# Band attention: queries and keys transposed by Vector and transfers in place of TensorE, in a new order

## The chip, the cores and the metric

The kernel runs on one core of a Trainium2 chip. The metric is device time in microseconds (us), the median of several runs. Five engines work side by side, each through its own list of instructions in order: TensorE (PE in the profile; PEld is its weight load), VectorE (DVE), ScalarE (ACT), GpSimd (POOL) and SyncE (SP), which here only issues transfers (DMAs). They wait for each other through semaphores. SBUF is the working memory of 128 partitions; PSUM is the accumulator memory, eight banks of 2 KB per partition, where TensorE writes.

## The reference

The reference is a decoder of twelve stages over 32 sequences of 128 tokens with 128 features. Only the last stage changes. It is six layers of local attention, each followed by a gated feed-forward block:

```python
for i in range(DEPTH):                                   # 6
    x = attn_layer(shift_tokens(x), Wqkv[i], q_scale[i], k_scale[i], Wo[i]) + x
    x = ffn_layer(shift_tokens(x), ln_g[i], ln_b[i], W1[i], b1[i], W2[i], b2[i]) + x
```

In `attn_layer` the tokens are projected to queries, keys and values of 16 heads of 64; queries and keys are divided by their norms, scaled per feature and turned by rotary tables; each token attends to a band of its own window and the one before; the softmax of 8 times the scores weighs the values; the result is projected to 128 features. In `ffn_layer` a layer norm is followed by two projections to 341 columns, one passed through Gelu and multiplied with the other, and a projection back.

The score matmul contracts over the 64 features of a head, so queries and keys must lie with features on the partitions. The projections leave them with tokens on the partitions. They have to be transposed in between, and this step is what changes.

## The kernel before

The stage is `l3_ffn` of class `Fast` (from line 1818). An item n is one sequence in one layer: 6 x 32 = 192 items. The residual stream is `Z`, kept in SBUF throughout. The loop runs over t, and in each iteration every step works on another item: `steps` lists the functions with their lag, so that `(scores, 3)` in iteration t is the score step of item t - 3. The feed-forward block works on four items at once (a group g), so its functions in `blocks` come up in one of four iterations: `ff_gates` when t mod 4 is 0, `ff_up` and `ff_norm` when it is 1, `ff_down` and `ff_normed` at 2, `ff_turn` at 3. The text calls these four the gates, up, down and turn iterations; `shifted`, the transpose of the next four inputs, falls in the last. In the first layer the functions in `ahead` finish the stage before.

The order of the list is the order of the work on each engine. `Ordered` and `Lane` (lines 1332 to 1360) tie every compute instruction to the one before it on the same engine, so no engine overtakes; transfers are not tied. Every compute instruction goes through `Lane`, which is why the profile gives L1345 for all of them and groups have to be told apart by tile names.

The steps of an item are these, with the tile names that the profile shows.

- `queries(n, w)` multiplies the shifted input `zs` with 1024 columns of the weights, for queries (w = 0) and keys (w = 1), into a PSUM tile `qk`.
- `squares` squares it on ACT into `sq`; `summed` adds up the squares per head on DVE into `ss`. `sq` has one buffer.
- `swapped` and `rotated` read `qk` on DVE: one product with swapped halves into `rt`, one with the cosine table into `raw`; POOL adds the two in `raw`.
- `scaled`, an iteration later, makes the reciprocal roots of the sums (DVE, then 12 small POOL operations) and multiplies `raw` with them on POOL.
- `turned`, lag 2, transposes `raw` in 16 blocks of 128x128 on TensorE into PSUM tiles `rT`, four blocks to a tile; each tile is copied to SBUF as `qkT`, alternately by ACT and DVE. It stands in the list in two halves.
- `scores` fills two PSUM tiles `sc`. `hidden` first writes the band mask into all four banks of both with 16 small matmuls; 32 score matmuls add to it, and ACT takes the exponential into `P`.
- `valued` projects values (`vp`, copied to `va`); `values` multiplies `P` with them (`av`) and divides on DVE into `ao`; `features` transposes `ao` (`oTp`, then `oT`); `projected` multiplies with the output weights (`y`), and DVE adds to `Z`.
- `ff_norm` shifts by a matmul (`hp`), copies into `zh` and takes statistics; `ff_normed` normalises; `ff_turn` transposes (`xp`) into `xT`; `ff_gates` makes three projections (`gp`) and their Gelu (`g`); `ff_up` three more (`ap`) and the products `u`; `ff_down` projects back (`fy`).

PSUM is divided between two pools. The first holds three tiles of two banks for `qk`, `sc`, `av` and `vp`; the second two tiles of one bank for everything else. `zh` and `xT` are two names in one single buffer:

```python
p2 = es.enter_context(tc.tile_pool(name="L3fp2", bufs=3, space=PSUM))
p1 = es.enter_context(tc.tile_pool(name="L3fp1", bufs=2, space=PSUM))
...
zh = wk.tile([128, 4, 128], F32, tag="zh", name="zh", bufs=1)
...
xT = wk.tile([128, 512], F32, tag="zh", name="xT", bufs=1)
```

A tile of a pool is given its buffer when the last access to the buffer's former tile is over. Accesses of different engines to the same PSUM bank of one tile are kept apart, reads too. `weights` loads a layer's weights over SP's queue and builds the table `tab`.

Of the kernel before, what the change touches and what calls it, by code (L numbers as in the profile page):

```python
# [13 lines left out]
F32 = mybir.dt.float32  # L14
# [10 lines left out]
S = 128  # L25
# [1336 lines left out]
class Fast(General):  # L1362
# [455 lines left out]
    def l3_ffn(self):  # L1818
        if self.general:
            return super().l3_ffn()  # L1820
        tc, i, plain = self.tc, self.i, self.nc
        nc = self.nc = Ordered(plain, tc)
        N = DEPTH * NB
        with ExitStack() as es:
# [112 lines left out]

            def weights(l):
                wqkv = wt.tile([128, 3072], F32, tag="wqkv", name="wqkv")
                nc.sync.dma_start(out=wqkv, in_=i["dqkv"][l])  # L1940
                wo = wt.tile([128, 8, 128], F32, tag="wo", name="wo")
                nc.sync.dma_start(out=wo, in_=i["dwo"][l])
                w1 = wt.tile([128, 682], F32, tag="w1", name="w1")
                nc.sync.dma_start(out=w1, in_=i["dw1"][l])
                w2 = wt.tile([128, 3, 128], F32, tag="w2", name="w2")
                nc.sync.dma_start(out=w2, in_=i["dw2"][l])
                dqs = wt.tile([1, 256], F32, tag="dqs", name="dqs", bufs=1)
                nc.sync.dma_start(out=dqs, in_=i["dqs"][:, 256 * l:256 * l + 256])
                p = bank([128, 256], "tabp")
                mm(p, self.ones, dqs)  # L1950
                tab = wt.tile([128, 2, 2, 64], F32, tag="tab", name="tab")
                nc.vector.tensor_tensor(tab.rearrange("p w c d -> p (w c d)"), p, rot, ALU.mult)
                rs = wt.tile([128, NB, 16], F32, tag="rs", name="rs")
                W[l] = (wqkv, wo, w1, w2, tab, rs)

            def shifted(g):

                p = bank([128, 4, 128], "zT")
                for j in range(4):
                    turn(p[:, j, :], Z[:, 4 * (g % 8) + j, :])  # L1960
                zs = zs2[g % 2]
                nc.scalar.copy(zs[0:64], p[0:64])
                nc.vector.tensor_copy(zs[64:128, :, 1:128], p[64:128, :, 0:127])

            def queries(n, w):
                x = zs2[n // 4 % 2][:, n % 4, :]
                if w == 0:
                    S[n] = {"raw": wk.tile([128, 32, 64], F32, tag="raw", name="raw", bufs=3),
                            "ss": wk.tile([128, 32], F32, tag="ss", name="ss")}
                pp = banks([128, 16, 64], "qk")  # L1970
                for u in range(2):
                    c = 1024 * w + 512 * u
                    mm(pp[:, 8 * u:8 * u + 8, :], x, W[n // NB][0][:, c:c + 512])
                S[n]["qk"] = pp
# [30 lines left out]
                rn = self.rsqrt(wk, v, "s", nc.gpsimd)  # L2005
                nc.gpsimd.tensor_tensor(s["raw"], s["raw"], rn.unsqueeze(2).to_broadcast([128, 32, 64]), ALU.mult)

            def turned(n, us):
                s = S[n]
                flat = s["raw"].rearrange("p h d -> p (h d)")  # L2010
                if us[0] == 0:
                    s["qkT"] = wk.tile([128, 16, 128], F32, tag="qkT", name="qkT")
                for u in us:
                    p = bank([128, 4, 128], "rT")
                    for c in range(4):
                        o = 512 * u + 128 * c
                        turn(p[:, c, :], flat[:, o:o + 128])
                    (nc.vector.tensor_copy if u % 2 else nc.scalar.copy)(s["qkT"][:, 4 * u:4 * u + 4, :], p)

            def valued(n):  # L2020
                vp = banks([128, 16, 64], "vp")
# [4 lines left out]

            def scores(n):
                s = S[n]
                qkT = s["qkT"]

                sc = [banks([128, 2, 4, 128], "sc") for _ in range(2)]
                self.hidden(mm, [sc[f][:, e].rearrange("p c q -> p (c q)") for f in range(2) for e in range(2)],
                            self.bandT)
                s["P"] = []
                for f in range(2):
                    for c in range(4):
                        for e in range(2):
                            r = slice(64 * e, 64 * e + 64)
                            mm(sc[f][:, e, c, :], qkT[r, 8 + 4 * f + c, :], qkT[r, 4 * f + c, :], start=False, stop=c == 3)
                    P = wk.tile([128, 8, 128], F32, tag="P", name="P", bufs=4)  # L2040
                    nc.scalar.activation(P.rearrange("p h q -> p (h q)"), sc[f].rearrange("p e c q -> p (e c q)"), AF.Exp,
                                         scale=8.0)
                    s["P"].append(P)
# [40 lines left out]
            def ff_norm(g):  # L2084
                b = slice(4 * (g % 8), 4 * (g % 8) + 4)
                p = bank([128, 4, 64], "hp")
                mm(p, self.bg("shift"), Z[:, b, 64:128])
                zh = wk.tile([128, 4, 128], F32, tag="zh", name="zh", bufs=1)
                nc.gpsimd.tensor_copy(zh[:, :, 0:64], Z[:, b, 0:64])
                nc.scalar.copy(zh[:, :, 64:128], p)  # L2090
                mv = wk.tile([128, 4, 2], F32, tag="fmv", name="fmv")
                for j in range(4):
                    st = self.sp.tile([128, 6], F32, tag="bnst", name="bnst")
                    nc.vector.bn_stats(st, zh[:, j, :])
                    nc.vector.bn_aggr(mv[:, j, :], st)
                v = wk.tile([128, 4], F32, tag="fv", name="fv")
                nc.vector.tensor_scalar(v, mv[:, :, 1], EPS, None, ALU.add)
                rn = self.rsqrt(wk, v, "f", nc.gpsimd)
                nb = wk.tile([128, 4], F32, tag="fnb", name="fnb")
                nc.gpsimd.tensor_tensor(nb, mv[:, :, 0], rn, ALU.mult)  # L2100
                nc.gpsimd.tensor_scalar(nb, nb, -1.0, 0.0, ALU.mult, ALU.add)
                F[g] = {"xn": zh, "nb": nb, "rn": rn, "gs": [], "u": []}

            def ff_normed(g):
                zh, nb, rn = F[g]["xn"], F[g]["nb"], F[g]["rn"]
# [20 lines left out]
                    nc.scalar.activation(t[0:m], gp[0:m], AF.Gelu, bias=self.col(f"L3f_b1{l}1{c}")[0:m])  # L2126
                    F[g]["gs"].append((t, m))

            def ff_up(g):
                l = g // 8  # L2130
                w1, xT = W[l][2], F[g]["xT"]
                for c, (t, m) in enumerate(F[g]["gs"]):
                    ap = bank([128, 512], "ap")
                    mm(ap[0:m], w1[:, 128 * c:128 * c + m], xT)
                    u = uc if c == 2 else wk.tile([128, 512], F32, tag=f"u{c}", name=f"u{c}", bufs=1)
                    nc.vector.scalar_tensor_tensor(u[0:m], ap[0:m], self.col(f"L3f_b1{l}0{c}")[0:m], t[0:m],
                                                   ALU.add, ALU.mult)
                    F[g]["u"].append(u)

            def ff_down(g):  # L2140
# [10 lines left out]
                if l == DEPTH - 1:  # L2151
# [3 lines left out]

            weights(0)
            ahead = ((normed, 3), (x_values, 5), (x_scores, 6), (x_keys, 7), (x_turn, 8), (x_norm, 9), (x_root, 10))
            steps = ((features, 5), (summed, 1, 1), (scaled, 1), (queries, 0, 0), (squares, 0), (swapped, 0, 0),
                     (rotated, 0, 0), (turned, 2, (0, 1)), (scores, 3), (summed, 0, 0), (turned, 2, (2, 3)),
                     (queries, 0, 1), (squares, 0), (swapped, 0, 1), (rotated, 0, 1), (projected, 5), (values, 4))  # L2160
            blocks = ((ff_normed, 7), (ff_turn, 8), (ff_down, 11), (ff_up, 10), (ff_gates, 9), (ff_norm, 6))
            for t in range(-10, N + 12):
                if 0 <= t < N and t % NB == NB - 4 and t // NB + 1 < DEPTH:
                    weights(t // NB + 1)
                for fn, lag, *a in steps:
                    if 0 <= t - lag < N:
                        fn(t - lag, *a)
                for fn, lag in blocks:
                    n = t - lag
                    if n % 4 == 3 and 0 <= n < N:  # L2170
                        fn(n // 4)
                for fn, at in ahead:
                    n = t + at
                    if n % 4 == 0 and 0 <= n < NB:
                        fn(n // 4)
                if t % 4 == 3 and 0 <= t + 1 < N:
                    shifted((t + 1) // 4)
                if 0 <= t - 2 < N:
                    valued(t - 2)
# [888 lines left out]
```

## Time and profile before

| | |
|---|---|
| median of three runs | 6189.32 us (6188.6 to 6194.51) |
| the profiled execution | 6190.12 us |
| its span, first to last instruction | 6188.2 us |
| mean granted TensorE clock | 0.941 |
| the band layers, first query projection to the last | 2745 to 6094 us |

A line of the groups or of the timeline names the source line, the engine, the operation and the tiles as out<-in, then the shape and the count. In the groups, "busy, mean ns" follow, then the engine's idle time just before such instructions and what ended it. In the timeline the first two numbers are start and duration in us, and square brackets hold the idle time before. A line of the waits says who waited for whom, for how many us in total, how often, and the longest. In the table of windows each engine's busy time stands with its instruction count, then the granted clock.

Matmuls are pipelined: the start of the next one says how long one holds the engine, not its own duration. An fp32 matmul has two records per call.

### The profile page before, as it was taken

What the parts mean: (1) busy time and instruction counts of PE and PEld (TensorE: products, weight loads), DVE (VectorE), ACT (ScalarE), POOL (GpSimd) and SP (SyncE); (2) the same over time, 40 slices, a digit from 0 to 9 for tenths busy, and PEclk for the clock granted to TensorE, in tenths of its full rate; (3) what the DMA queues carried; (4) which work ended last, traced back from release to release, by engine and by line L of the source; (5) the groups of instructions that cost most, each with busy time, mean ns of one, the idle gap of its engine ahead of it and who ended that gap; (6) DMA issues with size and microseconds to landing.
All of it is one profiled execution on the core that took longest, in us unless ns stands there. A gap on an engine that the chain in (4) does not pass through costs nothing.

```text
span 6188.2 us, 144055 instructions
## 1 busy us (share of the span) xinstructions
PE 5484.6 (89%) x59686; PEld 3895.3 (63%) x59686; DVE 4046.0 (65%) x11606; ACT 2984.4 (48%) x4283; POOL 3083.4 (50%) x4828
## 2 busy tenths in 40 slices
PE   8867957868859999868999999999999999999998
PEld 4534546755646666646666666666666666666766
DVE  5576532345549999957666666666666676666664
ACT  6756611114435555524555554554555555554554
POOL 0141010011025555547766666666666667666774
PEclk9988966768989999989999999999999999999999
DMA  1000057533012212200000000000000000000000
GB/s 44 2 1 1 2 202 260 169 93 106 5 28 55 55 47 54 55 28 5 5 17 15 5 1 1 15 5 2 12 8 2 1 15 5 2 2 1 3 6 9
DMA packets 243639, 208.11 MB, mean 34 GB/s; under 512 B 125746, under 2 KB 230809, under 8 KB 237854
## 3 DMA queue, kind: packets, MB, share of 16 engines
q1 hardware_dynamic: 239372, 162.06, 9.1%
q0 software_dynamic: 2304, 33.56, 1.4%
q8 instruction: 471, 7.72, 0.5%
q10 hardware_dynamic: 1298, 3.19, 0.1%
q14 instruction: 194, 1.59, 0.1%
HBM read 140.83 MB, written 57.93 MB: 32 GB/s over the span
## 4 chain that ended last, share of the span: by engine, by line
PE 37%; DVE 21%; ACT 6%; issue 3%; POOL 1%; DMA 1%; SPq 0%; DVEq 0%; ACTq 0%; POOLq 0%
PE qk L1345 8%; DVE rt L1345 5%; PE vp L1345 5%; DVE raw L1345 5%; PE av L1345 5%; PE y L1345 5%; ACT sq L1345 4%; PE gp L1345 3%; PE fy L1345 2%; PE oTp L1345 2%; PE rT L1345 2%; DVE qkT L1345 2%; DVE ss L1345 1%; DVE ao L1345 1%; PE tp L1345 1%
## 5 line engine op out<-in xcount | busy, mean ns | idle before, releaser
L1345 POOL TENSOR_TENSOR raw<-raw,rt 128x1024 f32<-128x1024 f32 x384 | 902.6, 2356 | 335.1 <-DVE raw L1345 335.1
L1345 DVE TENSOR_TENSOR rt<-qk,tab 128x1024 f32<-128x1024 f32 x384 | 470.3, 1225 | 879.1 <-ACT sq L1345 869.7
L1345 POOL TENSOR_TENSOR raw<-raw,ry 128x2048 f32<-128x2048 f32 x224 | 811.3, 3622 | 17.5
L1345 PE MATMUL qk<-wqkv,zs 128*128 128x512 f32 x1536 | 728.0, 597 | 3.0 <-DVE zs L1345 3.0
L1345 ACT ACTIVATE sq<-qk 128x1024 f32<-128x1024 f32 x448 | 459.3, 1025 | 536.6 <-PE qk L1345 404.3
L1345 POOL TENSOR_TENSOR rt<-ry 128x32 f32<-128x32 f32 (+1 forms) x864 | 198.3, 230 | 752.9 <-DVE ry L1345 644.1
L1345 DVE TENSOR_REDUCE ss<-sq 128x16 f32<-128x1024 f32 x448 | 539.3, 1209 | 48.9 <-ACT sq L1345 47.6
L1345 PE MATMUL rT<-ident,raw 128*128 128x128 f32 x3072 | 452.4, 280 | 89.0 <-DVE qkT L1345 77.4
L1345 PEld LDWEIGHTS rT<-ident,raw 128*128 128x128 f32 x3072 | 341.5, 141 | 258.8 <-DVE qkT L1345 122.3
L1345 DVE TENSOR_TENSOR raw<-qk,tab 128x1024 f32<-128x1024 f32 x384 | 466.5, 1215 | 0.0
L1345 ACT ACTIVATE PT<-sc 128x1024 f32<-128x1024 f32 x384 | 373.1, 1028 | 138.3 <-PE sc L1345 138.0
L1345 ACT COPY va<-vp 128x1024 f32<-128x1024 f32 (+1 forms) x232 | 218.3, 941 | 453.2 <-PE vp L1345 453.0
L1345 PEld LDWEIGHTS y<-wo,oT 128*128 128x128 f32 x3072 | 372.8, 192 | 91.5 <-issue 78.7
L1345 ACT ACTIVATE P<-sc 128x1024 f32<-128x1024 f32 x384 | 372.3, 1022 | 114.9 <-PE sc L1345 114.3
L1345 PE MATMUL av<-va,P 128*64 128x65 f32 x12288 | 401.0, 223 | 0.0
L1345 PE MATMUL sc<-qkT 64*128 64x128 f32 x6144 | 394.6, 278 | 0.0
L1345 PEld LDWEIGHTS av<-va,P 128*64 128x64 f32 x12288 | 374.3, 137 | 23.8 <-issue 0.8
L1345 PEld LDWEIGHTS sc<-qkT 64*128 64x128 f32 x6144 | 357.9, 188 | 43.6 <-issue 43.6
L1345 PEld LDWEIGHTS qk<-wqkv,zs 128*128 128x128 f32 x1536 | 264.1, 192 | 192.3 <-issue 188.4
L1345 PE MATMUL y<-wo,oT 128*128 128x128 f32 x3072 | 374.4, 275 | 1.4 <-DVE qkT L1345 0.8
L1345 PE MATMUL vp<-wqkv,zs 128*128 128x512 f32 x768 | 362.9, 595 | 0.7 <-DVE rs L1345 0.7
L1345 POOL TENSOR_TENSOR X<-X,brep 128x512 f32<-128x512 f32 x24 | 30.5, 1271 | 526.4 <-DVE xn L1345 526.4
(421 smaller groups left out, 11412.2 us busy)
## 6 DMA issues: line engine op xcount, KB each, us to landing
rows<-scr SPq DMA_DIRECT2D x32, 672.0 KB
tup<-whole SPq DMA_DIRECT2D x8, 2048.0 KB
gt<-tup SPq DMA_DIRECT2D x64, 256.0 KB
tdn<-whole SPq DMA_DIRECT2D x8, 2048.0 KB
gd<-tdn SPq DMA_DIRECT2D x128, 128.0 KB
T<-flt SPq DMA_DIRECT2D x16, 1024.0 KB
wqkv<-in_dqkv SPq DMA_DIRECT2D x6, 1536.0 KB
scr<-dots SPq DMA_DIRECT2D x128, 66.0 KB
```

The lines of the kernel that those rows point to most:

```text
L1345: self.last = call(*a, **k)
```

## The change

`turned` no longer uses TensorE. DVE transposes the keys' half and then the queries' half of `raw` within blocks of 32x32 into a tile `bt1` or `bt0` (one buffer each). A full transpose also has to bring block row j and block column a to each other's place; for each pair (a, j), SP issues one transfer from 32 partitions of `bt` to 32 partitions of `kT` or `qT`: 16 for the keys, 16 for the queries. For the keys each partition's 1 KB is written as eight pieces of 128 bytes, for the queries as one piece. The PSUM tiles `rT` and the copies to `qkT` are gone; `scores` reads `kT` and `qT`.

The list of steps is rearranged, and the feed-forward functions stand inside it. The key projection and the feed-forward work now come before `scores`. The sum of squares of the queries comes before their rotation. `ff_up` is split: two thirds before `ff_norm`, the last third after `scores`. The statistics of `ff_norm` become `ff_stats`, the last step. Three smaller edits: the weights are loaded over ACT's queue, the second `zs` copy moves from DVE to ACT and the first `zh` copy from POOL to ACT, and `raw` has two buffers in place of three.

```diff
             def weights(l):
                 wqkv = wt.tile([128, 3072], F32, tag="wqkv", name="wqkv")
-                nc.sync.dma_start(out=wqkv, in_=i["dqkv"][l])
+                nc.scalar.dma_start(out=wqkv, in_=i["dqkv"][l])
...
-                nc.vector.tensor_copy(zs[64:128, :, 1:128], p[64:128, :, 0:127])
+                nc.scalar.copy(zs[64:128, :, 1:128], p[64:128, :, 0:127])
...
-                    S[n] = {"raw": wk.tile([128, 32, 64], F32, tag="raw", name="raw", bufs=3),
+                    S[n] = {"raw": wk.tile([128, 32, 64], F32, tag="raw", name="raw"),
...
-            def turned(n, us):
-                s = S[n]
-                flat = s["raw"].rearrange("p h d -> p (h d)")
-                if us[0] == 0:
-                    s["qkT"] = wk.tile([128, 16, 128], F32, tag="qkT", name="qkT")
-                for u in us:
-                    p = bank([128, 4, 128], "rT")
-                    for c in range(4):
-                        o = 512 * u + 128 * c
-                        turn(p[:, c, :], flat[:, o:o + 128])
-                    (nc.vector.tensor_copy if u % 2 else nc.scalar.copy)(s["qkT"][:, 4 * u:4 * u + 4, :], p)
+            def turned(n):
+
+                raw = S[n]["raw"].rearrange("p h d -> p (h d)")
+                S[n]["kT"] = kT = wk.tile([128, 8, 128], F32, tag="kT", name="kT")
+                S[n]["qT"] = qT = wk.tile([128, 4, 8, 32], F32, tag="qT", name="qT")
+                for w, dst in ((1, kT.rearrange("p c (j k) -> p j c k", j=4)), (0, qT)):
+                    bt = wk.tile([128, 4, 8, 32], F32, tag=f"bt{w}", name=f"bt{w}", bufs=1)
+                    nc.vector.transpose(bt, raw[:, 1024 * w:1024 * w + 1024].rearrange("p (c a d) -> p a c d", c=8, a=4))
+                    for a in range(4):
+                        for j in range(4):
+                            nc.sync.dma_start(out=dst[32 * a:32 * a + 32, j], in_=bt[32 * j:32 * j + 32, a])
...
-                            mm(sc[f][:, e, c, :], qkT[r, 8 + 4 * f + c, :], qkT[r, 4 * f + c, :], start=False, stop=c == 3)
+                            mm(sc[f][:, e, c, :], kT[r, 4 * f + c, :], qT[r, 4 * f + c], start=False, stop=c == 3)
...
-                nc.gpsimd.tensor_copy(zh[:, :, 0:64], Z[:, b, 0:64])
+                nc.scalar.copy(zh[:, :, 0:64], Z[:, b, 0:64])
                 nc.scalar.copy(zh[:, :, 64:128], p)
+                F[g] = {"xn": zh, "gs": [], "u": []}
+
+            def ff_stats(g):
+                zh = F[g]["xn"]
...
-            def ff_up(g):
+            def ff_up(g, lo, hi):
                 l = g // 8
                 w1, xT = W[l][2], F[g]["xT"]
-                for c, (t, m) in enumerate(F[g]["gs"]):
+                for c in range(lo, hi):
+                    t, m = F[g]["gs"][c]
...
-            steps = ((features, 5), (summed, 1, 1), (scaled, 1), (queries, 0, 0), (squares, 0), (swapped, 0, 0),
-                     (rotated, 0, 0), (turned, 2, (0, 1)), (scores, 3), (summed, 0, 0), (turned, 2, (2, 3)),
-                     (queries, 0, 1), (squares, 0), (swapped, 0, 1), (rotated, 0, 1), (projected, 5), (values, 4))
-            blocks = ((ff_normed, 7), (ff_turn, 8), (ff_down, 11), (ff_up, 10), (ff_gates, 9), (ff_norm, 6))
+            steps = ((1, features, 5), (1, turned, 2), (1, summed, 1, 1), (1, scaled, 1), (1, queries, 0, 0), (1, squares, 0),
+                     (1, summed, 0, 0), (1, swapped, 0, 0), (1, rotated, 0, 0), (4, ff_normed, 7), (4, ff_turn, 8),
+                     (4, ff_down, 11), (4, ff_up, 10, 0, 2), (4, ff_gates, 9), (4, ff_norm, 6), (1, queries, 0, 1),
+                     (1, squares, 0), (1, swapped, 0, 1), (1, rotated, 0, 1), (1, scores, 3), (4, ff_up, 10, 2, 3),
+                     (1, projected, 5), (1, values, 4), (4, ff_stats, 6))
```

The other loads of `weights` move to ACT's queue in the same way. In the loop, each entry runs when its item n is in range and n mod `per` is `per` - 1.

More of the change, by code (lines that the diff above doesn't have):

```diff
@@ L1939, in weights @@
                 wqkv = wt.tile([128, 3072], F32, tag="wqkv", name="wqkv")
-                nc.sync.dma_start(out=wqkv, in_=i["dqkv"][l])
+                nc.scalar.dma_start(out=wqkv, in_=i["dqkv"][l])
                 wo = wt.tile([128, 8, 128], F32, tag="wo", name="wo")
-                nc.sync.dma_start(out=wo, in_=i["dwo"][l])
+                nc.scalar.dma_start(out=wo, in_=i["dwo"][l])
                 w1 = wt.tile([128, 682], F32, tag="w1", name="w1")
-                nc.sync.dma_start(out=w1, in_=i["dw1"][l])
+                nc.scalar.dma_start(out=w1, in_=i["dw1"][l])
                 w2 = wt.tile([128, 3, 128], F32, tag="w2", name="w2")
-                nc.sync.dma_start(out=w2, in_=i["dw2"][l])
+                nc.scalar.dma_start(out=w2, in_=i["dw2"][l])
                 dqs = wt.tile([1, 256], F32, tag="dqs", name="dqs", bufs=1)
-                nc.sync.dma_start(out=dqs, in_=i["dqs"][:, 256 * l:256 * l + 256])
+                nc.scalar.dma_start(out=dqs, in_=i["dqs"][:, 256 * l:256 * l + 256])
                 p = bank([128, 256], "tabp")
@@ L2028, in scores @@
                 s = S[n]
-                qkT = s["qkT"]
+                kT, qT = s["kT"], s["qT"].rearrange("p j c k -> p c j k")
                 sc = [banks([128, 2, 4, 128], "sc") for _ in range(2)]
@@ L2101, in ff_norm @@
                 nc.gpsimd.tensor_scalar(nb, nb, -1.0, 0.0, ALU.mult, ALU.add)
-                F[g] = {"xn": zh, "nb": nb, "rn": rn, "gs": [], "u": []}
+                F[g].update(nb=nb, rn=rn)
             def ff_normed(g):
@@ L2164, in l3_ffn @@
                     weights(t // NB + 1)
[L2165 to L2168, printed above, removed]
+                for per, fn, lag, *a in steps:
                     n = t - lag
-                    if n % 4 == 3 and 0 <= n < N:
-                        fn(n // 4)
+                    if 0 <= n < N and n % per == per - 1:
+                        fn(n // per, *a)
                 for fn, at in ahead:
```

## The prediction

> **What bounds the kernel now.** I read the busy totals, then busy time in windows of the band layers, then the waits there, then the timeline of four items.
>
> ```profile
> PE 5484.6 (89%) x59686; PEld 3895.3 (63%) x59686; DVE 4046.0 (65%) x11606; ACT 2984.4 (48%) x4283; POOL 3083.4 (50%) x4828
> ...
> L1345 DVE TENSOR_REDUCE ss<-sq 128x16 f32<-128x1024 f32 x448 | 539.3, 1209 | 48.9 <-ACT sq L1345 47.6
> L1345 PE MATMUL rT<-ident,raw 128*128 128x128 f32 x3072 | 452.4, 280 | 89.0 <-DVE qkT L1345 77.4
> ```
> ```profile
> 4000.00:4200.00 200.00, 193.94 (x2026) 138.22 (x2026) 137.69 (x230) 104.26 (x141) 136.59 (x218) 1.00 0.01 4
> ```
> The window shows, in order, PE, weight loads, DVE, ACT, POOL, granted clock, DMA share and GB/s. TensorE is busy 97% at full clock; Vector and Pool have a third to spare, the DMA engines nearly everything. TensorE sets the pace.
>
> Starts of first-query projections in the timeline (4014.03, 4031.66, 4050.24, 4067.76, 4083.50) give the four kinds of iteration: gates 17.63, up 18.58, down 17.52, turn 15.74; sum 69.47, mean 17.37. 192 items take 3335 us of the profiled 6190.12 (span 6188.2).
>
> ```profile
> 4014.03 1.88 PE L1345 MATMUL qk<-wqkv,zs 128*128 128x512 f32 x4
> ...
> 4015.75 1.04 PE L1345 MATMUL rT<-ident,raw 128*128 128x128 f32 x8
> ...
> 4015.99 1.02 ACT L1345 ACTIVATE sq<-qk 128x1024 f32<-128x1024 f32 x1 [0.65 <-ACT oT L1345]
> ...
> 4017.12 1.22 DVE L1345 TENSOR_TENSOR rt<-qk,tab 128x1024 f32<-128x1024 f32 x1 [2.06 <-ACT sq L1345]
> ...
> 4018.26 1.21 DVE L1345 TENSOR_TENSOR raw<-qk,tab 128x1024 f32<-128x1024 f32 x1
> ...
> 4020.13 0.66 PE L1345 MATMUL rT<-ident,raw 128*128 128x128 f32 x4 [0.41 <-DVE qkT L1345]
> ```
> From the first projection to the end of "raw" is 5.44 us, and only then is that item's query bank pair free. Vector's swap waits for ACT's squares, which read the same banks. Today transposes and scores fill those microseconds.
>
> ```profile
> POOL zh L1345 <- PE ap L1345: 38.9, 28, 1.4
> ```
> In the waits, zh is overwritten only after the last "ap" matmul: zh and xT share one buffer.
>
> **What the skill says.** "VectorE: DVE Perf Modes", The three transpose paths: Vector transposes only 32x32 blocks, 311 ns for 128x128 bf16. "Vector Engine (DVE) Microarchitecture Reference", 3.8: one element per cycle per lane. No transpose on Vector is in this trace; the 1024-element operations at 1209 to 1225 ns are the nearest rows. "TensorE: Matmul & The Clock Gate", Part 1: the array clock halves after an idle window of about 3.4 us. The trace agrees, and shows that the window need not be wholly idle (an earlier stage; PE busy first, clock third from the right):
> ```profile
> 2168.96:2172.38 3.42, 0.91 (x5) 0.47 (x4) 3.42 (x17) 1.61 (x2) 3.01 (x6) 1.00 0.01 2
> 2172.38:2175.79 3.41, 3.29 (x14) 2.33 (x12) 3.41 (x23) 1.66 (x3) 3.41 (x8) 0.50 0.00 0
> 2175.79:2179.20 3.41, 3.41 (x35) 3.29 (x36) 3.41 (x28) 1.59 (x4) 3.32 (x3) 1.00 0.00 0
> ```
> A window with 0.91 us of work is followed by one at half clock.
>
> **The change, part by part.** Removed per item: 16 TensorE transposes. In the timeline they hold TensorE from 4015.75 to 4016.71 and from 4019.06 to 4020.62, waits included: 2.5 us. Also four copies, two on Vector (0.68) and two on ACT (0.59).
>
> Added: two Vector transposes of 128x1024 at the head of the iteration. The rows of 692 ns for 512 elements (ao) and 1225 for 1024 (rt) give 533 ns per 512, so 1.07 us is the lower bound; 2.3 the upper, if four-byte data passes twice. I take 1.2, so 2.4 per item.
>
> Added: 32 transfers per item on SP. Nearest row, an earlier stage:
> ```profile
> 1779.33 7.83 SPq L2326 DMA_DIRECT2D scr<-dots  x16
> 1789.54 0.34 SPq L2329 DMA_DIRECT2D rows<-scr  x1
> ```
> That is 0.49 us apiece (median of one 0.38), and the load that needs them starts 2.4 us after the last. So 32 cost 12 to 15.7 us, against items of 16 to 21 us. The scores that read them come more than an iteration later: hidden. Each transposed tile has one buffer, so Vector's next transpose waits until its 16 transfers have landed: an item can't be shorter than 32 issues + 2.5 us, 14.7 to 18.2. I take the lower half, hidden; at the top end it just binds, and behind that transpose stand the reduce, the squares and the masks.
>
> Moved, and this decides: both projections now run ahead of the scores. The pool has three bank pairs; first queries, second queries and two score tiles are four. The band masks, first of the score matmuls, touch both score tiles, so they wait until "raw" of the first queries is done. In Vector's order the reduce (1.21) now precedes the swap: 5.44 + 1.21 = 6.65, and TensorE resumes at 6.7. TensorE times per piece, from the timeline: projection 1.71, masks .37, scores 1.98, y 1.87, av 2.03, vp 1.71, oTp .87, seams .2.
>
> - turn: 1.71 + .43 (xp) + 1.71 = 3.85, wait 2.85 to 6.7; then .37 + 1.98 + 1.87 + 2.03 + .43 (zT) + 1.71 + .87 + .2 = 16.2, before 15.74.
> - gates: two gp to 3.43; the third needs a bank freed by the first Gelu, which now follows the squares (2.98) and a 1.28 table load, ending 4.95: wait 1.6. Third gp and projection to 7.6, past 6.7, no mask wait: + 9.03 = 16.6, before 17.63.
> - up: two ap to 3.43; hp needs a bank freed by the first product u, now behind "raw" on Vector: 6.65 + .74 = 7.4, wait 4.0. hp and projection to 9.5, masks and scores to 11.9, third ap to 12.75. ACT's copies into zh stand ahead of the second squares and the exponentials, and wait for this ap; y waits for zh to free hp's bank (13.7) and ends 15.6. The second squares end at 14.7, "raw" at 17.2, the exponentials at 16.6: av waits, between 0.1 and 1.6 us for its first half. 20.5 to 22.0; I take 20.9, before 18.58.
> - down: the layer-norm statistics (2.3: four pairs of 270 + 182 ns, three of 170) now stand before the two transposes (2.4) and the old reduce (1.2) on Vector, after the last ao (1.15 past av): 7.0 past av, 4.4 past the first projection, and the squares have one buffer, which that reduce frees. Squares to 5.5, reduce, swap, raw to 9.1. TensorE: 1.71 + 2.76 (fy) + 1.71 = 6.2, wait 2.95; + 9.03 = 18.2, before 17.52.
>
> Sum 71.9 against 69.47: +2.4 per four items, x 48 = +115 us. Put otherwise: TensorE's work is 59.0 per four, so break-even is a mean wait of 2.6 us per item; I find 3.2.
>
> The clock: three of four iterations now have a hole of 2.85 to 4.0 us, about one clock window. Each should bring at least one window at half clock: at most 1.7 us lost in one, up to 3.4 if a second stays low. I take 1.5: 3 x 1.5 x 48 = +216.
>
> At nothing: weight loads moved to ACT's queue (five issues of 0.33 per layer, buffers free long before; without ACT's idle half 10 us); the zs copy (0.69) from Vector to ACT; "raw" with two buffers, whose reader is earlier in Vector's own order. The stores of the last layer (SP waits for Pool's X, eight times) now stand before transfers on SP: 0 to 40 us, taken as 0. Pool loses the 0.4 us zh copy.
>
> 6190 + 115 + 216 = 6521, rounded to 6520; the profiled run is within 1 us of the median.
>
> **Rivals.**
> 1. Holes as above, clock holds: 6305. For: windows above half busy mostly kept it. Against: a hole of 4 us cannot avoid a poor window.
> 2. Vector or the transfers become the bound. Transposes of 2.3 us add 2.2 us where Vector is late (turn, up, down) and 1.3 at gates: 7.9 x 48 = +380, 6900. The point is Vector's slack in the turn kind, some 0.5 us. Issues of 0.6 us make items 19.2 + 2.5 = 21.7 us, + 4.3 x 192, 7020.
> 3. Faster: the bank wait isn't there. If the masks got their banks before "raw", turn loses 2.85 and down 2.95: 66.1 per four, -162, 6030, with no large hole but hp's. It decides for faster below a mean wait of 2.6 us. For: TensorE's own work shrinks by 15% (59.0 against 69.5). Against: three bank pairs, four live tiles.
> 4. The change doesn't do what it says: the transposes leave TensorE by construction, so only the order's effect is open.
>
> **How the numbers follow.** Likeliest case (clock drops) 0.47, own range 6400 to 6680; rival 1 0.18; rival 2 0.18; rival 3 0.13; 0.04 for a balance within 0.2%, about what a measurement here can tell from no change. Slower: 0.47 + 0.18 + 0.18 = 0.83. Range 6190 to 7050: below lies most of rival 3, above the case of slow transposes and slow transfers together.
>
> **What would show it.** Right: rT gone; "sc" (masks) waiting on DVE raw, hp on DVE u, ACT zh on PE ap; granted clock under 0.95 in the band layers; TensorE busy near 80% there; transposes near 1.2 us; SP issuing 32 in under 16 us. Wrong: TensorE still over 95% busy with shorter items, or full clock despite holes, or PE waiting on DMA kT, qT.

## The result, and the profile after

The changed kernel takes 7287.24 us, median of four runs (7281.09 to 7294.38), against 6190.34 (6188.6 to 6194.51) for the kernel before, measured beside it: a ratio of 1.177, 95% interval 1.1753 to 1.1785. The profiled execution took 7292.79 us, its span is 7291.0, the mean granted clock 0.863 where it was 0.941.

The first and the fifth part of the page of the changed kernel (busy totals; groups as out<-in, shape, count, busy, mean ns, idle before and what ended it):

```profile
PE 5614.2 (77%) x56614; PEld 3857.5 (53%) x56614; DVE 4253.3 (58%) x11558; ACT 2835.3 (39%) x3995; POOL 3070.0 (42%) x4780
...
L1345 DVE STREAM_TRANSPOSE bt<-raw 128x1024 f32<-128x1024 f32 x384 | 470.9, 1236 | 559.1 <-DMA qT<-bt 531.9
```

The 3072 TensorE transposes (`rT`, 452.4 us of busy time) are gone: 56614 matmul records in place of 59686. Yet TensorE's busy time rose, from 5484.6 to 5614.2: a matmul at half clock holds the engine longer, and the score matmuls take longer even at full clock (both are shown at the kernels with 16 transfers). A Vector transpose takes 1.24 us, as assumed. New is the end of the line: before transposing, Vector stood idle for 559 us, and 532 of them ended with a transfer from `bt` to `qT`.

The same 500 us of both kernels in the table of windows (PE, weight loads, DVE, ACT, POOL, clock, DMA share, GB/s), before and then after:

```profile
4000.00:4500.00 500.00, 485.45 (x5077) 347.24 (x5076) 343.08 (x574) 254.85 (x344) 344.44 (x535) 1.00 0.02 6
```
```profile
4000.00:4500.00 500.00, 377.61 (x3367) 252.79 (x3366) 279.78 (x423) 175.44 (x227) 251.44 (x398) 0.85 0.24 52
```

After the change TensorE is busy 76%, Vector 56%, Pool 50%, ACT 35%, the DMA engines 24%. No compute engine is full, and the DMA engines are idle three quarters of the time. The bound must be something that this view has no column for. It is SP, which computes nothing and whose issuing isn't counted as busy. The instructions on tile `bt` (durations are minimum, median and maximum in ns, then the first and last start) and who waited:

```profile
L2018 SPq DMA_DIRECT2D kT<-bt x3072: 585/609/2285, 2768.9 to 7225.3; - x192
L2018 SPq DMA_DIRECT2D qT<-bt x3072: 507/589/1940, 2779.5 to 7236.3; - x192
L1345 DVE STREAM_TRANSPOSE bt<-raw x384: 1201/1245/1248, 2767.6 to 7216.5; 128x1024 f32<-128x1024 f32 x192
...
  DVE bt L1345: 544.6, 148
  PEld sc L1345: 7.0, 20
  PE sc L1345: 1.7, 4
```

From one issue to the next it is 0.652 us (median of all 6144, from the trace), 0.664 on average without the 128 intervals over 1.5 us. 32 of them are 21.2 us; the items follow each other at 23.15. The waits by TensorE for transfers are nothing (8.7 us): the data do come in time. It is the release of `bt`, the place they are taken from, that comes too late. The timeline shows the circle:

```profile
4502.23 10.69 SPq L2018 DMA_DIRECT2D qT<-bt  x16
...
4511.63 1.23 DVE L1345 STREAM_TRANSPOSE bt<-raw 128x1024 f32<-128x1024 f32 x1
...
4513.03 10.44 SPq L2018 DMA_DIRECT2D kT<-bt  x16
...
4514.37 1.25 DVE L1345 STREAM_TRANSPOSE bt<-raw 128x1024 f32<-128x1024 f32 x1 [1.50 <-DMA qT<-bt]
...
4520.15 1.22 DVE L1345 TENSOR_TENSOR raw<-qk,tab 128x1024 f32<-128x1024 f32 x1
...
4522.08 1.22 PE L1345 MATMUL hp<-Z,c_big 128*128 128x256 f32 x2 [5.12 <-DVE u L1345]
...
4523.56 11.10 SPq L2018 DMA_DIRECT2D qT<-bt  x16
...
4530.77 0.40 ACT L1345 COPY zh<-Z 128x256 f32<-128x256 f32 x1 [12.91 <-PE ap L1345]
...
4541.12 4.33 SPq L2018 DMA_DIRECT2D kT<-bt  x6
```

The last of the 16 query transfers is issued by 4512.92 and has landed by 4514.37, when Vector may write the query half of `bt` again. Behind that transpose stand the reduce, the swap, `raw` and the products `u`; TensorE waits 5.12 us for `u`. The keys' 16 follow the queries' at 4513.03 without a gap, since the keys have a tile `bt` of their own, and the queries' follow these at 4523.56.

Those end at 4534.66, and then SP stands idle until 4541.12. The next transposes come late there: they are at the head of a down iteration, and in the trace Vector reaches them at 4539.80, behind the last third of `u` and the layer-norm statistics. Over the whole stage three of four items begin on SP 21.7 to 21.8 us after the one before, and the fourth 27.8 us after it (medians, from the trace); with the old order, tried below, the fourth follows after 22.7. So the issues alone set the pace for three items, and at the fourth a delay from the new order comes on top.

The three waits that were forecast are there too (waits from 3700 to 6000 us, lines of ACT, PE, DVE and PEld). Those of the masks and of `hp` are longer than without the bound: 5.4 and 5.9 us each, where the kernel with 16 transfers below has 2.7 and 3.6.

```profile
ACT zh L1345 <- PE ap L1345: 303.7, 24, 13.2
...
PE sc L1345 <- DVE raw L1345: 270.0, 50, 9.4
DVE bt L1345 <- DMA qT<-bt: 267.9, 72, 7.0
...
PEld hp L1345 <- DVE u L1345: 162.4, 24, 8.0
```

### The profile page after: what moved, and what is told of

It is laid out like the page before. It is cut to its first block, busy times and chain, and to the rows that moved or that the text cites. A ratio compares the mean times of both kernels' runs of the same rounds, so it can differ in the third digit from the quotient of the medians.

```text
span 7291.0 us, 146878 instructions
## 1 busy us (share of the span) xinstructions
PE 5614.2 (77%) x56614; PEld 3857.5 (53%) x56614; DVE 4253.3 (58%) x11558; ACT 2835.3 (39%) x3995; POOL 3070.0 (42%) x4780
## 3 DMA queue, kind: packets, MB, share of 16 engines
q14 instruction: 251, 2.06, 0.1%
## 5 line engine op out<-in xcount | busy, mean ns | idle before, releaser
L1345 PE MATMUL qk<-wqkv,zs 128*128 128x512 f32 x1536 | 846.0, 680 | 10.6 <-DVE raw L1345 9.0
L1345 DVE STREAM_TRANSPOSE bt<-raw 128x1024 f32<-128x1024 f32 x384 | 470.9, 1236 | 559.1 <-DMA qT<-bt 531.9
L1345 PE MATMUL sc<-qT,kT 64*128 64x128 f32 x6144 | 615.6, 347 | 4.6 <-DMA qT<-bt 1.7
L1345 PEld LDWEIGHTS sc<-qT,kT 64*128 64x128 f32 x6144 | 562.9, 253 | 85.7 <-issue 70.1
L1345 PE MATMUL sc<-bandT,identh 32*32 32x512 bf16 x3072 | 144.1, 491 | 540.3 <-DVE raw L1345 540.3
L1345 PEld LDWEIGHTS <-identh 32*32 32x32 bf16 (+1 forms) x4224 | 59.1, 91 | 800.7 <-DVE raw L1345 569.7
L1345 PEld LDWEIGHTS qk<-wqkv,zs 128*128 128x128 f32 x1536 | 319.9, 223 | 306.8 <-issue 296.4
L1345 PE MATMUL y<-wo,oT 128*128 128x128 f32 x3072 | 424.7, 295 | 35.5 <-ACT zh L1345 35.3
L1345 PEld LDWEIGHTS y<-wo,oT 128*128 128x128 f32 x3072 | 388.3, 205 | 99.5 <-ACT zh L1345 75.0
```

The lines of the kernel that those rows point to most:

```text
L1345: self.last = call(*a, **k)
```

## The experiments

Periods are medians of the distance between the starts of the first query projections, by kind of iteration, over the items from the 49th on, and the mean is that of all items; the last column is the share of the time in which the records of the granted clock stand at half, without the two ends of the stage. Both are worked out from the traces. All kernels made from the changed one keep its three smaller edits; no run has these alone, so their share is not known.

| kernel | median, us | ratio to before (95%) | gates | up | down | turn | mean | half clock |
|---|---|---|---|---|---|---|---|---|
| before | 6190 | | 17.63 | 18.59 | 17.52 | 15.74 | 17.49 | 0 |
| changed | 7287 | 1.1769 (1.1753 to 1.1785) | 22.97 | 25.30 | 20.98 | 24.02 | 23.15 | 0.29 |
| new order, TensorE transposes | 6960 | 1.1242 (1.1223 to 1.1261) | 20.30 | 26.48 | 19.08 | 21.06 | 21.50 | 0.09 |
| old order, 32 transfers | 7077 | 1.1433 (1.1414 to 1.1452) | 22.90 | 24.08 | 18.23 | 21.61 | 21.95 | 0.26 |
| new order, 16 transfers | 6621 | 1.0695 (1.0677 to 1.0712) | 17.34 | 22.93 | 20.95 | 18.12 | 19.75 | 0.16 |
| old order, 16 transfers | 6104 | 0.9858 (0.9842 to 0.9875) | 17.14 | 18.11 | 17.23 | 14.59 | 17.03 | 0.01 |

### The order alone

The changed kernel, with the `turned` of before in one piece:

```diff
-(1, turned, 2),
+(1, turned, 2, (0, 1, 2, 3)),     # 16 transposes on TensorE, four copies to qkT
```

> The new order with the transposes still on TensorE (16 blocks at the head of each iteration, copies on ACT and DVE as before): no transfers and no Vector transposes. Theory A (SP's transfers set the pace of the changed kernel, 32 issues of 0.66 us and a landing, some 23 us an item): with SP idle the time falls far below 7287, to what the new order costs by itself; from the walk of the prediction plus 1.7 us of transposes an item, holes and slower clock included, 6650 to 6850 us. Theory B (the order and its holes explain the whole loss, the transfers are hidden): stays at 7200 or above.

It took 6960.32 us, between the two ranges. The order, with the smaller edits, costs 768 us by itself (6192 for the kernel before, measured beside it), and it is not the whole: the change costs 1097. The sum of four items is 86.0 (4 x 21.50). That is the 69.5 us that four items took before, TensorE 97% busy, the 12.9 us of holes of the prediction's walk (71.9 - 59.0), and 3.6 us for the clock and the rest. I had set the range too low by not adding all holes to the full work.

### The transfers alone

The changed kernel, with the steps in the order of before. `turned` stays at the head, the statistics stay a step of their own, and the smaller edits stay (the diff is shortened):

```diff
-steps = ((1, features, 5), (1, turned, 2), (1, summed, 1, 1), (1, scaled, 1), (1, queries, 0, 0), (1, squares, 0),
-         (1, summed, 0, 0), (1, swapped, 0, 0), ...
+steps = ((1, features, 5), (1, turned, 2), (1, summed, 1, 1), (1, scaled, 1), (1, queries, 0, 0), (1, squares, 0),
+         (1, swapped, 0, 0), (1, rotated, 0, 0), (1, scores, 3), (1, summed, 0, 0), (1, queries, 0, 1), ...
```

> The old order of steps with Vector transposes and all 32 transfers an item. Theory A: an item can't be shorter than 32 x 0.66 + 2.5 = 23.6 us, so 192 items take about 4500 us and the time stays at 7200 to 7450 whatever the order. Theory B: without the new order's bank waits the time returns to 6190 or below.

It took 7076.67 us: theory A in kind, some 120 us below its range. Theory A had added 2.5 us for the landing to 32 issues; the mean period of 21.95 us is shorter than that sum, 23.6, and 0.7 us longer than the issues alone. Without the new order's holes, Vector waits for transfers twice as long as in the changed kernel, and now the scores do as well (tile `bt`, who waited):

```profile
  DVE bt L1345: 1049.6, 213
  PE sc L1345: 501.5, 185
  PEld sc L1345: 448.0, 144
```

The two costs, 768 and 884, don't add up to the 1097 of the whole: both are limits on the same iteration, and the longer one covers part of the other.

### Half as many transfers, the same bytes

One tile `bt` for both halves, and one transfer for each pair (a, j) that carries queries and keys together, 64 KB in place of 32 (the code is shortened):

```diff
-for w, dst in ((1, kT...), (0, qT)):
-    bt = wk.tile([128, 4, 8, 32], ...)
-    nc.vector.transpose(bt, raw[...])
-    for a, j: nc.sync.dma_start(out=dst[32 * a:32 * a + 32, j], in_=bt[32 * j:32 * j + 32, a])
+bt = wk.tile([128, 4, 16, 32], F32, tag="bt", name="bt", bufs=1)
+for w in (1, 0):
+    nc.vector.transpose(bt[:, :, 8 * w:8 * w + 8], raw[...])
+for a, j: nc.sync.dma_start(out=qkT[32 * a:32 * a + 32, :, 32 * j:32 * j + 32], in_=bt[32 * j:32 * j + 32, a])
```

> The changed kernel with 16 transfers an item in place of 32, each carrying the key block and the query block together (64 KB, same bytes in all, sixteen pieces of 128 bytes per partition). Theory A with a fixed price per transfer: 16 x 0.66 = 10.6 us, no longer the bound; the time falls to the holes and the clock, 6450 to 6650 us. If the price of a transfer goes with its bytes or pieces (1.3 us each): stays near 7287. Theory B: stays near 7287 too, so the issue time of one transfer in the trace tells the last two apart: 0.66 us or 1.3 us.

It took 6620.95 us, as theory A expected. So 666 us of the loss go with the number of transfers. Twice the bytes cost nearly the same per issue, 0.672 us from start to start in place of 0.652 (medians), and Vector no longer waits (tile `bt`):

```profile
L2018 SPq DMA_DIRECT2D qkT<-bt x3072: 585/627/3002, 2762.5 to 6558.5; - x192
...
  DVE bt L1345: 1.7, 1
```

What is left is the kernel that my forecast had in mind. The holes and the clock can be seen one behind the other in its timeline of TensorE, the down iteration:

```profile
4522.16 0.39 PE L1345 MATMUL sc<-bandT,identh 32*32 32x512 bf16 x2
4525.74 0.65 PE L1345 MATMUL sc<-bandT,identh 32*32 32x512 bf16 x14 [3.19 <-DVE raw L1345]
4526.32 4.12 PE L1345 MATMUL sc<-qkT 64*128 64x128 f32 x32
```

Two masks run, the other 14 wait 3.19 us for `raw`, and the scores that follow take 4.12 us; in the gates and up iterations beside it, at full clock, they take 2.39 and 2.46.

The same edit in the old order:

> Old order, Vector transposes, 16 transfers an item. Theory A with a fixed price per transfer: neither SP nor a bank wait binds and TensorE has 2.5 us less an item; 6050 to 6200 us, the first version that may beat the kernel before. With a price by bytes: 7200 or above. Theory B: 6190 or below.

It took 6104.24 us, 1.4% less than the kernel before, as expected. So Vector's transposes with 16 transfers are a gain, the 32 transfers and the new order are the two losses. From the kernel before: -88 for the transposes taken off TensorE (with the smaller edits), +517 for the order, +666 for twice as many transfers, together 1095. These parts hold for this way from one kernel to the other: the order costs 768 us with TensorE's transposes, 517 with 16 transfers and 211 with 32.

A part of what the transposes free goes to the scores. The group of the score matmuls in the kernel before, and in this one, which is at half clock for 0.01 of the time:

```profile
L1345 PE MATMUL sc<-qkT 64*128 64x128 f32 x6144 | 394.6, 278 | 0.0
```
```profile
L1345 PE MATMUL sc<-qkT 64*128 64x128 f32 x6144 | 477.2, 282 | 15.7 <-DMA qkT<-bt 9.4
```

The same matmuls hold TensorE 83 us longer, 0.43 us an item: a set of 32 takes about 2.46 us at full clock in place of 2.06. With TensorE's transposes in the new order it takes 2.06, and in the kernel before with extra transfers (next section) the group stays at 394.6. So it goes neither with the order nor with transfers beside it, but with scores that read tiles written by transfers. What in that takes the time was not tried.

### What a transfer costs, by shape

The kernel before, with transfers between two otherwise unused tiles on SP's queue, in a new first step:

```diff
+(extra, 2),     # 16 (in layer 3: 4) transfers ddst<-dsrc per item, read by nobody
```

> The kernel before, with transfers between two otherwise unused SBUF tiles added on SP's queue, once per item, read by nobody; nothing else is changed. Their shape differs by layer: layer 1, 16 of 32 partitions x 1 KB; layer 2, 16 of 128 partitions x 256 B (same 32 KB); layer 3, 4 of 128 partitions x 1 KB (128 KB); layer 4, 16 of 64 partitions x 512 B; layer 5, 16 of 16 partitions x 2 KB; layer 6, 16 of 32 partitions x 8 pieces of 128 B. Theory A (a transfer has a price of its own on the issuing queue, some 0.65 us, whatever its shape): start to start 0.6 to 0.7 us in all six layers, the time within 0.5% of 6190, since 16 x 0.65 = 10.4 us fit into an item of 17.5 us. Theory B (the price goes by partitions): 0.3 to 0.4 us with 16 partitions, 0.65 with 32, 1.3 with 64, 2.6 with 128.

They wait for nothing in the loop, so SP ran ahead of it and had issued them all by 4843 us; the six shapes follow one another in time. The instructions on `ddst` in the stretches of the shapes 1, 2, 3 and 5 (32, 128, 128 and 16 partitions; 32, 32, 128 and 32 KB):

```profile
L1960 SPq DMA_DIRECT2D ddst<-dsrc x509: 507/589/1822, 2711.3 to 3098.9; - x170
...
L1960 SPq DMA_DIRECT2D ddst<-dsrc x510: 464/600/1942, 3103.7 to 3494.0; - x170
...
L1960 SPq DMA_DIRECT2D ddst<-dsrc x127: 464/601/1831, 3497.4 to 3639.9; - x127
...
L1960 SPq DMA_DIRECT2D ddst<-dsrc x510: 507/588/1668, 4036.9 to 4432.5; - x170
```

Within a burst the start-to-start medians are 0.633, 0.644, 0.643, 0.639, 0.632 and 0.653 us in the six shapes. Theory A holds: on this queue a transfer between SBUF tiles costs 0.63 to 0.65 us, whether it moves 32 or 128 KB, over 16 or 128 partitions, in pieces of 128 bytes or of 2 KB. The next burst, which had to wait for the last one's landing, starts 1.9 to 2.3 us after the start of the last issue (medians of the six shapes). No run issued a part of the transfers from another engine: whether the price belongs to SP, or to something that all queues share, stays open. The time is 6208.9 us, ratio 1.0024 (1.0017 to 1.0031): the 15 us stand in one single iteration, where `tab` of the next layer had to wait behind these transfers on SP's queue. All others have the period they had, within 0.11 us: the transfers as such disturb nobody.

### The buffer that zh and xT share

The kernel with the new order and 16 transfers, with

```diff
-xT = wk.tile([128, 512], F32, tag="zh", name="xT", bufs=1)
+xT = wk.tile([128, 512], F32, tag="xT", name="xT", bufs=1)
```

> The kernel with half as many transfers (6621 us), with a buffer of its own for xT, so that the new zh no longer waits for the last ap matmul, which now stands after the scores. Theory A (this wait of ACT, 302 us in the window from 3500 to 5500, holds up the second squares, the exponentials and y): the wait of zh on ap is gone, the up iterations shorten from 22.9 us by 1 to 3 us, the time is 6480 to 6580. Theory B (ACT has time to spare there and the up iteration is set by hp's wait for u alone): 6600 to 6640.

It took 6511.63 us, ratio 1.0515 (1.0498 to 1.0533), against 6620.95: 109 us less, theory A. The first `zh` copy no longer waits, the up iteration shrinks from 22.93 to 21.56. `hp` waits for `u` as long as before, 3.62 us. The same edit in the old order, where the last `ap` comes before `hp`:

> The kernel with the old order, Vector's transposes and 16 transfers (6104 us), with a buffer of its own for xT. ACT waited there 180 us for the last ap in the window from 3500 to 5500, ahead of the copies of va and oT. Theory A (the wait reaches TensorE): 6020 to 6085. Theory B (in this order the last ap comes early enough, and ACT's copies behind it are not late): 6090 to 6115, unless the pool then hands out its bank pairs in another turn, as with the second bt, where the time rose to 6177.

6105.41 us, ratio 0.9857 (0.9841 to 0.9874), against 6104.24: nothing. The wait of 180 us is only renamed, from `ap` to `hp` that follows it (183.1). Shared, the buffer costs nothing in the old order and 109 us in the new one, since there the third `ap` was moved behind the scores.

### What the half clock costs

The kernel with the new order and 16 transfers, with useless matmuls in the holes of two of the four kinds. They go to a bank that the masks then write over.

```diff
 sc = [banks([128, 2, 4, 128], "sc") for _ in range(2)]
+if n % 4 in (0, 3):
+    for _ in range(10):
+        mm(sc[0][:, 0], identh[0:32, 0, :], bandT[0:32, 0, :].unsqueeze(1).to_broadcast([32, 4, 128]))
```

> The kernel with half as many transfers (6621 us), with ten more bf16 matmuls (32 rows, 128 x 512 out, some 0.21 us each) into the first score bank ahead of the band masks, in the turn and the down iterations alone, where TensorE otherwise stands idle for 2.2 and 3.2 us until raw is done; the masks write over what they leave. TensorE gets 2.1 us of useless work in 96 items, which is 0.2 ms if nothing hides it. Theory A (the idle stretch costs twice, by itself and by the clock window at half speed after it): the share of half-clock time in the band layers, 0.156, falls below 0.12, the scores of the down iteration go from 4.1 to 2.5 us, and the time falls to between 6460 and 6560 although work was added. Theory B (the clock falls for other reasons): 6615 to 6660.

6615.21 us, ratio 1.0678 (1.066 to 1.0696): theory B by its number. The share at half clock went only from 0.156 to 0.126. But the trace shows more. Windows of this kernel in a turn iteration, along the edges of the clock's records (columns as above, the clock third from the right):

```profile
4533.68:4537.10 3.42, 3.36 (x31) 1.53 (x31) 3.42 (x4) 0.96 (x1) 2.93 (x7) 0.99 0.56 96
4537.10:4540.51 3.41, 3.41 (x31) 3.19 (x28) 0.95 (x1) 1.20 (x2) 3.41 (x2) 0.51 0.56 96
```

TensorE was busy for 3.36 of 3.42 us, and the window after it still came at half clock. All that ran in the first were added matmuls and masks over 32 rows of the array and then scores over 64. This window is not the only one. By the trace, 762 windows at full clock in the band layers were more than 90% busy in this kernel, and 19 of them were followed by half clock; without the added matmuls it was none of 658. So the same once more over all rows:

```diff
-mm(sc[0][:, 0], identh[0:32, 0, :], bandT[0:32, 0, :]...)
+mm(sc[0][:, 0], identh[:, 0, :], bandT[:, 0, :]...)
```

> The kernel with the filled hole (6615 us), in which the ten added matmuls contract over 128 rows in place of 32; their number, their output and their duration are the same. In the run with 32 rows the half-clock windows stayed, also one that followed a window in which TensorE was never idle but did only added matmuls of 32 rows, masks of 32 rows and scores of 64. Theory A (a window is judged by how much of the array works, so that matmuls of few rows count little): the share of half-clock time, 0.126 with 32 rows and 0.156 without the addition, falls below 0.09, the scores of the down and turn iterations take 2.4 to 2.6 us, and the time is 6480 to 6570. Theory B (the rows don't matter; the windows fall for another reason): the share stays at 0.11 to 0.14 and the time at 6600 to 6630.

6521.3 us, ratio 1.0526 (1.0507 to 1.0546), theory A. The share fell to 0.065, the down iteration from 20.80 to 19.37 us. In its timeline the hole is filled and the scores behind it run at full clock:

```profile
4560.72 2.64 PE L1345 MATMUL sc<-bandT,identh 128*128 128x512 bf16 x12
4564.39 0.43 PE L1345 MATMUL sc<-bandT,identh 32*32 32x512 bf16 x14 [1.02 <-DVE raw L1345]
4564.87 2.49 PE L1345 MATMUL sc<-qkT 64*128 64x128 f32 x32
```

The window in which the last five or six of the ten ran, and the one after it:

```profile
4561.68:4565.09 3.41, 2.33 (x25) 0.87 (x23) 3.41 (x5) 1.58 (x3) 2.73 (x9) 1.00 0.56 96
4565.09:4568.51 3.42, 3.40 (x42) 3.12 (x42) 2.10 (x2) 1.94 (x2) 3.42 (x2) 1.00 0.55 96
```

TensorE was busy for only 2.33 us of the first, 1.2 of them with 128 rows, and the clock stayed full. Of 766 windows over 90% busy in this kernel none was followed by half clock. The added matmuls take as long as the ones with 32 rows, and the two kernels differ in the rows alone: 94 us, 1.0 us for each of 96 items. The Trainium skill, "TensorE: Matmul & The Clock Gate", Part 1, says that the gate goes by how busy the array was in the last window of 3.4 us. These runs agree with the window (nearly all records at half clock last 3.41 us or a multiple of it) and add that busy is not the engine's time alone: the number of rows in use counts. By what measure it counts was not worked out.

### A second bt

The kernel with the old order and 16 transfers still had Vector wait for `bt`, so:

```diff
-bt = wk.tile([128, 4, 16, 32], F32, tag="bt", name="bt", bufs=1)
+bt = wk.tile([128, 4, 16, 32], F32, tag="bt", name="bt", bufs=2)
```

> The kernel with the old order, Vector's transposes and 16 transfers (6104 us), with two buffers for bt in place of one. There Vector waited for the last item's transfers before it could transpose anew, 223 us in the window from 3500 to 5500. Theory A (this wait passes on to TensorE through the rotations behind it): the wait is gone and the time falls to between 5980 and 6080. Theory B (Vector's slack takes it up): 6090 to 6115.

6176.81 us, ratio 0.9973 (0.9964 to 0.9983): neither theory, 73 us slower than with one buffer. The wait is gone, and gates and up shorten by 0.45 us each, but down goes from 17.23 to 19.75 (by the means of the whole stage, from 17.15 to 19.53). TensorE's waits from 3500 to 5500, with one buffer and with two:

```profile
PE qk L1345 <- ACT P L1345: 141.0, 117, 5.0
```
```profile
PE qk L1345 <- DVE raw L1345: 165.4, 115, 3.4
```

The key projection now waits for `raw` of the queries of the same item, where it waited for the exponentials: by these releasers it is handed the pair of banks of the first queries in place of that of a score tile. In a down iteration, where Vector is late, TensorE waits 3.05 us for it; with one buffer it waits 1.51 there. These waits differ by 24 us in 2000. A part of the rest is the clock, which stands at half for 0.04 of the time in place of 0.01. That the pool's choice of pair changed is read from the releasers; why a tile in SBUF should change it was not tried.

## Why the prediction was wrong

It said 6520 us, with 7050 as the upper end; 7287 is beyond it.

**The step that failed** is "Added: 32 transfers per item on SP", there "I take the lower half, hidden". The idea stood in it, that an item can't be shorter than its issues, and so did the rival "Issues of 0.6 us make items 19.2 + 2.5 = 21.7 us". The term that was mis-sized is the price of an issue: 0.38 to 0.49 us, taken from the one burst of 16 transfers in the trace of before (`scr<-dots`), which goes from SBUF to a tile in DRAM. Between SBUF tiles it is 0.66 on average, so 32 issues take 21.2 us, more than the 17.49 of an item before. They could not be hidden.

The other term of this bound, 2.5 us for the landing, was wrong too. Keys and queries have a tile `bt` each, so that the transfers of one are issued while those of the other land: on SP three of four items follow one another in 21.7 to 21.8 us, and the old order with 32 transfers has a mean of 21.95. That 32 x 0.66 + 2.5 = 23.6 comes near the 23.15 measured is luck. What fills the difference is the fourth item, for which SP waits until Vector has transposed. With the measured period, 6190 + (23.15 - 17.49) x 192 = 7277, which is the time within 10 us.

Of the signs that the prediction names, all of those for being right came but one: SP issues its 32 in 21.2 us and not in under 16. TensorE hardly waits for the transfers, 8.7 us in all, and the other two signs for being wrong did not show either; the wait went by way of Vector.

The Trainium skill, "DMA: Bandwidth & Descriptors", Latency and other measured facts, states some 600 ns to the first byte for this kind of queue, and its Rules for kernel authors advise to merge small transfers. Neither is a price per issue, but the first would have been the better guess, and the runs agree with the second: 16 double-sized transfers took SP half the time of 32 (16 x 0.672 = 10.8 us).

The chance given to the rival of slow transfers, 0.18 together with that of slow transposes, was low, and the upper end of the range lay 30 us above its time at 0.6 us, the dearest price considered. In a bound of 32 issues, 0.06 us more for one is 2 us for an item and 370 us for 192.

**Vector's transposes**: 1.2 us taken, 1.24 measured. Right; of the two bounds, 1.07 and 2.3, the lower was near.

**The holes.** The kernel with 16 transfers is the one that the sum was made for, and gives 6621 against the 6520 predicted. All forecast waits are in it: the masks for `raw` (3.19 us in the down iteration, 2.95 predicted; in the turn iteration 2.21, 2.85 predicted), `hp` for `u` (3.62, 4.0 predicted), the third `gp` for a Gelu (2.49, 1.6 predicted), `zh` for `ap` (302 us in 2000). The four items are 79.0 us (4 x 19.75); the walk gave 71.9 and 4.5 for the clock. 2.6 us per four are missing, 125 us in 48, of which 23 are an old mean set too low (17.37 for 17.49) and some 80 are the scores, which the walk took at their old 1.98 us. They are in all four kinds: 0.7 in gates, for which the walk had no clock loss, 0.5 in up, 1.25 in down, 0.4 in turn. "zh waits for the third ap" was priced at 0.1 to 1.6 us of the up iteration; the run without this wait shows 1.37 there and about 1 in down, 109 us in all.

**The clock.** Taken: 1.5 us for each of turn, up and down, "windows above half busy mostly kept it". Filling the holes of turn and down with matmuls over all rows gave 1.0 us each. The rival in which the clock holds is excluded: the share at half clock is 0.16 with 16 transfers, 0.29 with 32. That a window need not be idle to be followed by half clock was seen; that one which is 98% busy with few rows can be, was not.

**Rival 3**, with no wait for banks, fell: the masks wait for `raw` in every run of the new order.

**Faster than before** is possible with the idea itself: the old order with 16 transfers takes 6104 us.

## What to carry to other kernels

Before a step is turned into many small transfers, count them per iteration and multiply by the time of one issue on their queue, 0.65 us here, for all shapes tried; the result is a lower bound of the iteration that no busy column shows. Add a landing to it only where the next issue has to wait for one. Take the price from a burst of the same kind; where there is none, a tenth more per issue counts as often as there are issues, and the range must reach to it. When work is taken from the engine that sets the pace, keep the order that hid its waits: here the new order alone cost 768 us, and the removed transposes gained 88 in the old order.

## What the runs showed of the hardware

- A transfer between SBUF tiles issued by SP takes 0.63 to 0.67 us of that queue (medians), for 32 to 128 KB, 16 to 128 partitions and pieces of 128 bytes to 2 KB.
- A 3.4 us window in which TensorE is busy for 3.36 us with matmuls over 32 and 64 rows is followed by one at half clock, as are 19 of the 762 windows over 90% busy in that kernel; with 128-row matmuls in the same places it is none of 766, and the share of half clock goes from 0.126 to 0.065.
- The 32 score matmuls of an item take 2.46 us at full clock where they read tiles written by transfers, and 2.06 where ACT and DVE wrote them.
- A Vector transpose of 128x1024 four-byte elements in 32x32 blocks takes 1.24 us, as long as a product of that size (1.22).
